# Four-image hybrid network on one core: image 2's gating beside image 3's attention, its output projection in four blocks

## The chip, the cores and the metric

The kernel runs on one core of one Trainium2 chip. The core has four compute engines that each work through a queue of their own in order: PE (TensorE, matmuls into PSUM), DVE (VectorE), ACT (ScalarE) and POOL (GpSimd). A fifth, SP (SyncE), issues the DMAs here. The metric is the device time of one execution in microseconds (us). In what follows "image 3" is the last of four images (numbers 0 to 3).

## The reference, cut to what matters

Each of the 4 images is 1024 tokens of 256 channels. It passes layer 0 (norm, projection, 3x3 depthwise convolution, state-space scan with 64 states, norm, projection), layer 1 (three convolutions), layer 2 (masked attention with 8 heads, then a mixture of 8 experts) and layer 3 (state-space scan with 16 states and a gate, then a second mixture of experts). The change touches the parts below.

```python
# layer 2, attention: t = t + _L2_attn_ref(_ln_t(t), ...)
scores = jnp.where(mask, Q @ K.T / sqrt(32), -inf)
attended = softmax(scores) @ V
y = x + attended @ Wo + bo
out = layernorm(y) * gamma + beta
# layer 2, experts: t = t + _L2_ffn_ref(_ln_t(t), ...); 8 experts of 256 x 256 x 256, two best per token
# layer 3, second half of the scan layer (y from the scan over the tokens)
y = y * silu(x_gate)
t = t + y @ W_out + b_out
# layer 3, experts: t = t + _L3_ffn_ref(_ln_t(t), ...)
logits = xf @ gate_w + gate_b
probs = softmax(logits)
top2_vals, top2_idx = top_k(probs, 2)           # cw: weights of the two best, 0 elsewhere
for e in range(8):                              # 256 x 512 x 256 each
    h = gelu(xf @ W1[e] + b1[e])
    acc = acc + cw[:, e:e+1] * (h @ W2[e] + b2[e])
```

## The kernel before, in words

**Stages and scans.** The program is written out by one loop (`run`). It walks through the units of eight scans in the order of `SCANS`: (0,0), (0,1), (3,0), (0,2), (3,1), (0,3), (3,2), (3,3), where the first number is the layer and the second the image. One unit is 128 lanes by 1024 time steps: a load of `dt` into a buffer `dA`, an exponential on ACT, a matmul that spreads the input (`ps_rep`), a product and a scan on DVE into a buffer `h`, a product on POOL, and a matmul that collects the states (`ps_y`). The pool of the scans holds five buffers `dA`, five `h` and two `rows`, of which each scan takes one `rows`.

Between the units the loop advances the other work of the images as Python generators (`advance`): `front` (layer 0 up to its scan), `middle` (the rest of layer 0, layer 1, attention, layer 2's experts, and layer 3 up to its scan) and `last` (layer 3 behind its scan). Each `yield` is a point at which the loop may go back to the scan. So the order on every engine is fixed when the program is built.

**The end of the program.** The last scan, (3,3), needs image 3's `middle`. When the scan (3,2) has run out, `middle(3)` goes on without a scan beside it: attention's heads, the end of attention, layer 2's experts, and `front3`. Four empty units (`DRAIN`) keep the two scans apart.

**What runs beside it.** `ahead(2)` is image 2's layer 3 behind its scan: `back3` (gate and output projection), `moe(3, 2)` up to a mark `END` (norm, routing), and then its experts. In `middle(3)`, `beside(main, other)` alternates one step of `main` with one step of `other`. Before, `main` is only `moe(2, 3)`, image 3's layer-2 experts with their norm and routing. What is left of `ahead(2)` at its end is run up to `END` (`rest`), and the experts of image 2 come later, beside the last scan.

**Names to follow.** `back3` loads the residual rows into `tb_rows` (a `rows` buffer of the scans' pool), then for each of four blocks of 128 channels the gate (`gate_back`) and the scan's result (`y_back`), both in a pool of its own on the left side. POOL adds the bias to `tb_rows` in four instructions and multiplies `y_back` by the gate in eight (128 x 512 each). PE projects in four blocks of two token groups (`project(j)`, eight matmuls of 128 x 256, PSUM tile `ps_o3`, which the trace shows as `ps_o`), and DVE adds each block to `tb_rows` (`add(j)`).

The end of attention is `divided` (reciprocal on DVE, product on POOL, for each half of the channels of each half of the tokens), `projected` (`ps_wo`, added into `y_at`), and `normed` (statistics `lny`, then POOL's product with gamma and add into `tb`). `moe` begins with its norm (`lnm`, into `xnm`), its transposes (`ps_tr`), its logits (`ps_lg`), on POOL the adds `tb<-tb,xnm`, the routing on DVE (`lg`, `r_one`, `r_two`, `cw`), the weights turned (`ps_ct`) and the bias product (`ps_b`). Then comes the loop over the experts: `ps_h`, a gelu on ACT, `ps_e`, and an accumulation on DVE.

The side work shares three PSUM slots: `ps()` hands out the tags `s`, `s`, `acc` in turn, with two buffers of `s` and one of `acc`. When `self.alone` is set, the scores of the heads use the scans' PSUM instead.

Every operation passes through one metering helper, so the profile puts nearly all of them down to line 130; instructions are told apart by the names of their tiles (`x` in the trace is the buffer `x0`, used again for image 2's transposed rows).

Of the kernel before, what the change touches and what calls it, by code (L numbers as in the profile page):

```python
# [1 line left out]

# [14 lines left out]
P = 128  # L17
NB = 4
# [123 lines left out]
class Hybrid:  # L142
# [476 lines left out]
    def run(self):  # L619

        self.done, self.ready = set(), set()
        self.todo, self.stage, self.wait = list(STAGES), None, None
        self.alone, self.reached = False, 0
        nc, tc = self.nc, self.tc
        with tc.tile_pool(name="scan", bufs=1) as mp, tc.tile_pool(
            name="scps", bufs=1, space=PSUM
        ) as psum, tc.tile_pool(name="sdps", bufs=1, space=PSUM) as side, tc.manual_schedule():
            self.side_psum(side)
            self.scan_psum = psum
            self.mask_work, self.sorted = self.setup(), False  # L630
            clock = self.clock = dict.fromkeys(Metered.COST, 0.0)
            self.nc = Metered(nc, clock)
            for n, _ in enumerate(self.scans(mp, psum)):
                now = clock["vector"]
                if n % 2 and clock["gpsimd"] < now:
                    next(self.mask_work, None)
                for e in clock:
                    clock[e] = max(clock[e], now - LAG)
                for _ in range(TICKS):
                    if max(clock.values()) > clock["vector"] + LEAD or self.advance() is None:  # L640
                        break
            while self.advance() is not None:
                pass
            self.nc = nc
        assert not self.todo
# [269 lines left out]
    def scanned(self, key, y, d):  # L915

        yield Wait((key, d))
        for c in range(2):
            self.nc.sync.dma_start(y[64 * c : 64 * c + 64, d, :], self.mem["y", *key, d, c])

    def back0(self, b, tb):


        nc, tc, vec = self.nc, self.tc, self.vec
        with tc.tile_pool(name=f"k{b}", bufs=1, side="right") as sp:
            nc.sync.dma_start(tb, self.image(self.a["x"].rearrange("b h w c -> (b h w) c"), b))
            y = sp.tile([P, DC, L], F32, name="y_back")
            u = sp.tile([P, DC, L], F32, name="u_back")
            w_out = sp.tile([P, DC, C], F32, name="w_out0")

            def fetch(d):
                nc.sync.dma_start(u[:, d, :], self.mem["u", 0, b, d])
                yield from self.scanned((0, b), y, d)

            def skip(d):
                nc.vector.scalar_tensor_tensor(
                    y[:, d, :], u[:, d, :], vec["L0_conv_D_skip"][:, d : d + 1], y[:, d, :],
                    ALU.mult, ALU.add,
                )

            yield 1.0
            yield from fetch(0)
            yield from self.add_rows(tb, self.bout0, TB)
            nc.sync.dma_start(w_out, self.mem[("w_out0",)])
            for d in range(1, DC):
                yield from fetch(d)
                for _ in range(4):
                    yield 0.5
                skip(d - 1)
                yield 1.3  # L950
            for _ in range(4):
                yield 0.5
            skip(DC - 1)
            yield 1.3
            mv = sp.tile([P, TB, 2], F32, name="b0mv")
            got = {}

            def turn(j):
                got[j] = ps = self.ps("ps_yt")
                for d in range(DC):  # L960
                    nc.tensor.transpose(
                        ps[:, d * P : (d + 1) * P], y[:, d, j * P : (j + 1) * P], self.ident
                    )

            def stats(j):
                st = sp.tile([P, 6], F32, tag="b0st", name="b0st", bufs=2)
                nc.vector.bn_stats(st, got.pop(j))
                nc.vector.bn_aggr(mv[:, j, :], st)

            yield from self.pipe(range(TB), turn, stats, cost=1.0)  # L970
            r = self.rstd(sp, mv[:, :, 1], 1e-5, TB, "b0")
            yield 0.8

            def project(j):
                got[j] = ps = self.ps("ps_o")
                for d in range(DC):
                    nc.tensor.matmul(
                        ps[:, :C], lhsT=y[:, d, j * P : (j + 1) * P], rhs=w_out[:, d, :],
                        start=(d == 0), stop=(d == DC - 1),
                    )  # L980

            def add(j):
                nc.vector.scalar_tensor_tensor(
                    tb[:, j, :], got.pop(j)[:, :C], r[:, j : j + 1], tb[:, j, :], ALU.mult, ALU.add
                )

            yield from self.pipe(range(TB), project, add, cost=1.7)
# [275 lines left out]
    def attention(self, b, tb):  # L1263
        nc, tc, vec = self.nc, self.tc, self.vec
        with tc.tile_pool(name=f"at{b}", bufs=1, side="right") as op:
# [56 lines left out]
            with tc.tile_pool(name=f"ab{b}", bufs=1, side="right") as fp:  # L1322
                yield from self.shift(fp, qT, kT, mT, maskT, go, f"large{b}")
            with tc.tile_pool(name=f"ac{b}", bufs=1, side="right") as fp:
                yield from self.all_heads(fp, tb, qT, kT, v, maskT, mT, xa, wo)

    def all_heads(self, fp, tb, qT, kT, v, maskT, mT, xa, wo):
        nc = self.nc

        def divided(raw, sums, c):  # L1330
# [13 lines left out]
        for n in range(len(steps) + 2):  # L1344
# [13 lines left out]
            if n >= 2 and kb == TB - 1 and hp % 2:  # L1358
                then.append(divided(*halves[nh], hp // 2))
                if nh == 0 and hp == 3:  # L1360
                    then.append(self.finished(fp, tb, 0, halves[0][0], xa, wo, "s"))
        for more in then:
            yield from more
        yield from self.finished(fp, tb, 1, halves[1][0], xa, wo)

    def finished(self, fp, tb, nh, att, xa, wo, tag=None):
        y = yield from self.projected(fp, nh, att, xa, wo, tag)
        yield from self.normed(fp, tb, nh, y)

    def large_scores(self, fp, qT, kT, large):  # L1370
# [236 lines left out]
    def moe(self, which, b, tb, side="right", pause=False):  # L1607
# [8 lines left out]
        with ExitStack() as stack:  # L1616
# [22 lines left out]
            with tc.tile_pool(name=f"mg{which}{b}", bufs=1, side=side) as gp:  # L1639
                xn = gp.tile([P, TB, C], F32, name="xnm")  # L1640
                yield from self.norm(gp, tb, TB, xn, "lnm")
                yield from self.turned(xn, TB, xT)
                lg = gp.tile([P, TB, NEXP], F32, name="lg")
                ps = self.ps("ps_lg", (P, TB, NEXP))
                for j in range(TB):
                    for k in range(2):
                        nc.tensor.matmul(
                            ps[:, j, :], lhsT=xT[:, k, j * P : (j + 1) * P],
                            rhs=self.router[which][:, k, :], start=(k == 0), stop=(k == 1),
                        )  # L1650
                yield 3.0
                if which == 2:
                    nc.vector.tensor_copy(lg, ps)
# [5 lines left out]
                if which == 2:  # L1659
                    for j in range(0, TB, 2):  # L1660
                        tj = tb[:, j : j + 2, :]
                        nc.gpsimd.tensor_tensor(tj, tj, xn[:, j : j + 2, :], ALU.add)
                        yield 0.6
                yield from self.route(gp, lg, cw, which == 2)

                cT = gp.tile([NEXP, L], F32, name="cT")

# [26 lines left out]
            if pause:  # L1694
                yield END
                begin()
            hidden_of = {}
            got = {}

# [222 lines left out]
                    steps = self.beside(steps, self.other, lambda: ("parts", *key, 0) in self.ready)  # L1922
                yield from steps

    def back3(self, b, tb, side="right"):
        nc, tc = self.nc, self.tc
        with tc.tile_pool(name=f"h{b}", bufs=1, side=side) as sp:
            nc.sync.dma_start(tb, self.mem["t", b])
            y = sp.tile([P, DC, L], F32, name="y_back")
            gate = sp.tile([P, DC, L], F32, name="gate_back")  # L1930

            def fetch(d):
                nc.sync.dma_start(gate[:, d, :], self.mem["gate", b, d])
                yield from self.scanned((3, b), y, d)

            def gated(d):
                for g in range(2):
                    cols = slice(g * 512, (g + 1) * 512)
                    nc.gpsimd.tensor_tensor(y[:, d, cols], y[:, d, cols], gate[:, d, cols], ALU.mult)
                    yield 0.8  # L1940

            yield 1.0
            yield from fetch(0)
            w_out = self.weight(sp, "L3_attn_W_out", DC)
            yield from self.add_rows(tb, self.bout3, TB)
            for d in range(1, DC):
                yield from fetch(d)
# [8 lines left out]
            def project(j):  # L1956
                got[j] = ps = self.ps("ps_o3", (P, 2, C))
                for i in range(2):
                    m = 2 * j + i
                    for d in range(DC):  # L1960
                        nc.tensor.matmul(
                            ps[:, i, :], lhsT=y[:, d, m * P : (m + 1) * P], rhs=w_out[:, d, :],
                            start=(d == 0), stop=(d == DC - 1),
                        )

# [1 line left out]
                tj = tb[:, 2 * j : 2 * j + 2, :]  # L1967
                nc.vector.tensor_tensor(tj, got.pop(j), tj, ALU.add)

            yield from self.pipe(range(TB // 2), project, add, cost=3.4)  # L1970

# [37 lines left out]
    def middle(self, b):  # L2011

        with self.tc.tile_pool(name=f"t{b}", bufs=1, side="right") as tp:
            tb = tp.tile([P, TB, C], F32, name="tb")
            yield from self.back0(b, tb)
            yield from self.layer1(b, tb)
            yield from self.attention(b, tb)
            moe = self.moe(2, b, tb)
            if b < NB - 1:
                yield from moe  # L2020
            else:
                self.other = self.ahead(b - 1, "left", self.scan_pool)
                yield from self.rest((yield from self.beside(moe, self.other)))
            yield from self.front3(b, tb)

    def some(self, other, n):
# [28 lines left out]
    def ahead(self, b, side, pool=None):  # L2055

        with ExitStack() as stack:
            if pool is None:
                pool = stack.enter_context(self.tc.tile_pool(name=f"e{b}", bufs=2, side=side))
            tb = pool.tile([P, TB, C], F32, tag="rows", name="tb_rows", bufs=2 if pool is self.scan_pool else 1)  # L2060
            yield from self.back3(b, tb, side)
            yield from self.moe(3, b, tb, side, True)
            self.nc.sync.dma_start(self.image(self.out, b), tb)
            yield 1.0
# [60 lines left out]
```

## Time and profile before

| what | us |
|---|---|
| median of 3 timed runs (lowest, highest) | 6339.24 (6334.23, 6351.4) |
| the profiled execution | 6326.47 |
| its span | 6324.7 |
| PE busy (share) | 5136.2 (81%) |
| DVE busy (share) | 5039.6 (80%) |
| POOL busy (share) | 3824.8 (60%) |
| ACT busy (share) | 3410.2 (54%) |

The granted PE clock is 0.841 of full speed in the mean. The end of the execution divides like this (busy times from the trace, us):

| stretch | what runs | PE | DVE | POOL | clock |
|---|---|---|---|---|---|
| 5120 to 5238 | end of scan (3,2), image 3's attention up to its heads | 94.2 | 99.5 | 70.0 | 0.78 |
| 5240 to 5398 | image 3's heads, no scan | 155.6 | 14.4 | 9.5 | 1.00 |
| 5398 to 5459 | end of attention, norm and routing of the experts; image 2's fetches and gating | 29.2 | 25.9 | 26.0 | 0.58 |
| 5459 to 5601 | image 3's layer-2 experts; image 2's projection, norm and routing | 140.2 | 41.7 | 0.0 | 0.97 |
| 5601 to 5690 | `front3` of image 3 | 77.8 | 7.4 | 0.0 | 0.94 |
| 5690 to 6000 | scan (3,3), image 2's layer-3 experts | 274.4 | 252.9 | 192.9 | 0.95 |
| 6000 to 6324 | image 3's layer 3 to the end | 303.3 | 49.9 | 2.5 | 0.94 |

How to read it: a stretch is as long as the engine or the chain of waits that ends last in it, whatever the share over the whole span. An engine whose busy time comes near to the stretch's length sets it. Where none does, the length comes from instructions on different engines that wait for one another. The clock is the share of its full rate that PE was granted; a low one makes the same matmuls longer.

### The profile page before, as it was taken

Reading aid. Unit: us, or ns where it says so; the run is one execution under the profiler, and the core shown is the slowest. Engines: PE = TensorE matmul, PEld = TensorE weight load, DVE = VectorE, ACT = ScalarE, POOL = GpSimd, SP = SyncE. Lnnn points to the kernel's source line nnn. Section 1 sums busy time; section 2 is a strip of 40 time slices with the busy share of each in tenths; the row PEclk is TensorE's granted clock in tenths of the full one; section 3 lists DMA queues with packets and bytes.
Section 4 is the critical chain, followed back from the end, with each engine's and each line's share of the span. In section 5 each row is a group of like instructions: output and inputs, shape, how many; then the busy total and the mean of one; then the engine's idle time right before and its main releaser. Section 6 shows DMA issues by size and latency. Waiting matters only on the chain. (4 is left out here: it accounts for less than half of the span.)

```text
span 6324.7 us, 59731 instructions
## 1 busy us (share of the span) xinstructions
PE 5136.2 (81%) x20165; PEld 2118.7 (33%) x20249; DVE 5039.6 (80%) x4016; ACT 3410.2 (54%) x4299; POOL 3824.8 (60%) x1948
## 2 busy tenths in 40 slices
PE   6676785579798568979779969889689779797999
PEld 2222120132253022234225432243145332443566
DVE  5888898988898998889889988899889981317811
ACT  3565655345496435558637735577557544236621
POOL 2787768665686765668767756577857661106600
PEclk7687785589798568979869979989789889899989
DMA  3455555544355666445555675345545750226611
GB/s 110 158 159 165 164 175 187 157 150 133 120 172 178 195 166 164 129 131 187 161 176 181 181 177 158 119 150 195 188 146 175 203 150 11 53 73 179 171 34 34
DMA packets 347916, 934.97 MB, mean 148 GB/s; under 512 B 37748, under 2 KB 120257, under 8 KB 345985
## 3 DMA queue, kind: packets, MB, share of 16 engines
q1 hardware_dynamic: 344880, 928.38, 48.5%
q0 software_dynamic: 2128, 2.13, 0.2%
q8 instruction: 165, 2.70, 0.2%
q14 instruction: 167, 1.36, 0.1%
q10 hardware_dynamic: 576, 0.39, 0.0%
HBM read 841.02 MB, written 92.37 MB: 148 GB/s over the span
## 5 line engine op out<-in xcount | busy, mean ns | idle before, releaser
L130 POOL TENSOR_TENSOR h<-h,rows 128x1024 f32<-128x1024 f32 x1280 | 3023.4, 2365 | 1756.9 <-DVE h L130 1560.4
L130 DVE TENSOR_TENSOR_SCAN h<-dA,ps_rep 128x1024 f32<-128x1024 f32 x1280 | 2924.1, 2284 | 182.1 <-ACT dA L130 53.4
L130 DVE TENSOR_TENSOR ps_rep<-ps_rep,rows 128x1024 f32<-128x1024 f32 x1280 | 1549.0, 1210 | 145.6 <-PE ps_rep L130 144.6
L130 PE MATMUL ps_rep<-S,spread_L_conv_A_log 96*128 96x512 bf16 x2048 | 751.9, 456 | 771.7 <-DVE h L130 726.7
L130 ACT ACTIVATE dA<-dA,A_L_conv_A_log 128x1024 f32<-128x1024 f32 x1024 | 1125.6, 1142 | 442.5 <-DMA dA<-dt 414.0
L130 PE MATMUL ps_y<-h,collect_L_conv_A_log 128*32 128x512 f32 x4096 | 705.4, 742 | 15.5 <-POOL h L130 15.5
L130 PE MATMUL ps_e<-we,h_m 128*128 128x256 f32 x3072 | 709.2, 383 | 8.4 <-ACT h_m L130 8.4
L130 PEld LDWEIGHTS <-spread_L_conv_A_log 96*128 96x128 bf16 x2048 | 159.8, 102 | 1557.4 <-DVE h L130 1243.7
L130 PEld LDWEIGHTS ps_e<-we,h_m 128*128 128x128 f32 x3072 | 583.1, 191 | 159.2 <-issue 30.4
L130 PE MATMUL ps_h<-xTm,we 128*128 128x512 f32 x1280 | 603.3, 606 | 4.6 <-DMA we<-in_L_ffn_W_dram 4.5
L130 ACT ACT_TABLE_LOAD x402 | 515.8, 1283 | 37.6 <-PE ps_h L130 15.6
L130 ACT ACTIVATE h_m<-ps_h,cols 128x512 f32<-128x512 f32 x384 | 257.1, 686 | 437.7 <-PE ps_h L130 435.7
L130 ACT ACTIVATE p<-ps_sc 128x512 f32<-128x512 f32 x404 | 219.3, 595 | 319.7 <-PE ps_sc L130 215.2
L130 ACT ACTIVATE dA<-dA,A_L_attn_A_log 128x1024 f32<-128x1024 f32 x256 | 282.8, 1143 | 146.2 <-DMA dA<-dt 134.8
L130 PEld LDWEIGHTS ps_h<-xTm,we 128*128 128x128 f32 x1280 | 242.2, 193 | 279.2 <-issue 211.2
L130 PE MATMUL ps_rep<-S,spread_L_attn_A_log 96*128 96x512 bf16 x512 | 175.4, 430 | 158.2 <-DVE h L130 136.6
L130 PE MATMUL ps_at<-p,v 128*32 128x512 f32 x1024 | 271.5, 610 | 0.2 <-ACT p L130 0.2
L130 PE MATMUL ps_at<-p,ones 128*32 128x512 f32 x1024 | 271.5, 610 | 0.0
L130 PE MATMUL ps_sc<-qT,kT 32*128 32x512 f32 x808 | 244.5, 655 | 5.8 <-ACT p L130 3.5
L130 DVE SCALAR_TENSOR_TENSOR tb_rows<-ps_e,cw,tb_rows 128x256 f32<-128x256 f32 x128 | 55.7, 477 | 242.4 <-PE ps_e L130 242.2
L130 PE MATMUL ps_cv<-pad,diag 128*128 128x512 f32 x504 | 229.2, 594 | 0.0
L130 PEld LDWEIGHTS ps_y<-h,collect_L_conv_A_log 128*32 128x32 f32 x4096 | 93.9, 118 | 339.9 <-issue 224.3
(347 smaller groups left out, 5472.9 us busy)
## 6 DMA issues: line engine op xcount, KB each, us to landing
dA<-dt SPq DMA_DIRECT2D x1280, 512.0 KB
we<-in_L_ffn_W_dram SPq DMA_DIRECT2D x64, 512.0 KB
parts<-parts SPq DMA_DIRECT2D x60, 384.0 KB
S<-parts SPq DMA_DIRECT2D x90, 256.0 KB
dt<-sp_r SPq DMA_DIRECT2D x64, 256.0 KB
y<-yo SPq DMA_DIRECT2D x128, 128.0 KB
y_back<-y SPq DMA_DIRECT2D x64, 256.0 KB
we<-in_L_ffn_w_dram SPq DMA_DIRECT2D x64, 256.0 KB
```

Source lines behind the costliest of these rows:

```text
L130: return got(*args, **kw)
```

## The change

`middle` of the last image now starts `ahead(2)` beside attention and experts together instead of beside the experts alone. `back3` gets a `pause` mode for this. It first waits until the scan (3,2) has ended. Then it takes its `y_back` blocks and `W_out` from the five `h` buffers and its gate blocks from the `dA` buffers of the scans. The gating runs at once. The projection is cut into three groups, each held back by marks that image 3's work sets in `self.passed`: block 0 is issued when the last head is issued ("heads"), blocks 1 and 2 when attention's projection is ("projected"), block 3 when the logits are ("logits"). The adds of a group are issued when the mark "projected", "normed" or "routed" is set. Image 2's `moe(3, 2)` begins when image 3's loop over the experts begins ("route"). The load of `tb_rows` is issued when `ahead(2)` starts, that is behind attention's weights. `scanned` now takes a list of blocks, which changes nothing for layer 0.

```diff
@@ run, scanned @@
+        self.alone, self.reached, self.passed = False, 0, set()
...
-            self.nc.sync.dma_start(y[64 * c : 64 * c + 64, d, :], self.mem["y", *key, d, c])
+            self.nc.sync.dma_start(y[d][64 * c : 64 * c + 64, :], self.mem["y", *key, d, c])
@@ all_heads, finished, moe: the marks @@
+        self.passed.add(("heads", b))
         for more in then:
             yield from more
...
+        if nh:
+            self.passed.add(("projected", b))
         yield from self.normed(fp, tb, nh, y)
...
                 yield from self.norm(gp, tb, TB, xn, "lnm")
+                self.passed.add(("normed", b))
...
+                self.passed.add(("logits", b))
                 yield 3.0
...
                 yield from self.route(gp, lg, cw, which == 2)
+                self.passed.add(("routed", b))
...
             if pause:
                 yield END
                 begin()
+            self.passed.add(("route", b))
@@ back3 @@
-    def back3(self, b, tb, side="right"):
+    def back3(self, b, tb, side="right", pause=False):
...
             nc.sync.dma_start(tb, self.mem["t", b])
-            y = sp.tile([P, DC, L], F32, name="y_back")
-            gate = sp.tile([P, DC, L], F32, name="gate_back")
+            if pause:
+                yield Wait(((3, b), DC - 1))
+
+            def parts(name, tag):
+                if pause:
+                    return [
+                        self.scan_pool.tile([P, L], F32, tag=tag, name=name, bufs=5) for _ in range(DC)
+                    ]
+                x = sp.tile([P, DC, L], F32, name=name)
+                return [x[:, d, :] for d in range(DC)]
+
+            y, gate = parts("y_back", "h"), parts("gate_back", "dA")
...
-            w_out = self.weight(sp, "L3_attn_W_out", DC)
+            if pause:
+                w_out = self.scan_pool.tile([P, L], F32, tag="h", name="w_out3", bufs=5)
+                w_out = w_out.rearrange("p (k n) -> p k n", k=DC)
+                nc.sync.dma_start(w_out, self.a["L3_attn_W_out"].rearrange("(k p) n -> p k n", p=P))
+            else:
+                w_out = self.weight(sp, "L3_attn_W_out", DC)
...
-            yield from self.pipe(range(TB // 2), project, add, cost=3.4)
+            if pause:
+                for blocks, starts, ends in (
+                    ((0,), "heads", "projected"), ((1, 2), "projected", "normed"),
+                    ((3,), "logits", "routed"),
+                ):
+                    yield from self.until(starts, NB - 1)
+                    for j in blocks:
+                        project(j)
+                        yield 3.4
+                    yield from self.until(ends, NB - 1)
+                    for j in blocks:
+                        add(j)
+                        yield 0.5
+            else:
+                yield from self.pipe(range(TB // 2), project, add, cost=3.4)
+
+    def until(self, *what):
+        while what not in self.passed:
+            yield 0.0
@@ middle @@
-            yield from self.attention(b, tb)
-            moe = self.moe(2, b, tb)
             if b < NB - 1:
-                yield from moe
+                yield from self.attention(b, tb)
+                yield from self.moe(2, b, tb)
             else:
                 self.other = self.ahead(b - 1, "left", self.scan_pool)
-                yield from self.rest((yield from self.beside(moe, self.other)))
+                main = chain(self.attention(b, tb), self.moe(2, b, tb))
+                yield from self.rest((yield from self.beside(main, self.other)))
@@ ahead @@
-            yield from self.back3(b, tb, side)
+            yield from self.back3(b, tb, side, pool is self.scan_pool)
+            if pool is self.scan_pool:
+                yield from self.until("route", NB - 1)
             yield from self.moe(3, b, tb, side, True)
```

More of the change, by code (lines that the diff above doesn't have):

```diff
@@ L1 @@
 from contextlib import ExitStack
+from itertools import chain
 import concourse.bass as bass
@@ L622, in run @@
         self.todo, self.stage, self.wait = list(STAGES), None, None
-        self.alone, self.reached = False, 0
+        self.alone, self.reached, self.passed = False, 0, set()
         nc, tc = self.nc, self.tc
@@ L932, in fetch @@
                 nc.sync.dma_start(u[:, d, :], self.mem["u", 0, b, d])
-                yield from self.scanned((0, b), y, d)
+                yield from self.scanned((0, b), [y[:, k, :] for k in range(DC)], d)
             def skip(d):
@@ L1324, in attention, with all_heads @@
             with tc.tile_pool(name=f"ac{b}", bufs=1, side="right") as fp:
-                yield from self.all_heads(fp, tb, qT, kT, v, maskT, mT, xa, wo)
-    def all_heads(self, fp, tb, qT, kT, v, maskT, mT, xa, wo):
+                yield from self.all_heads(b, fp, tb, qT, kT, v, maskT, mT, xa, wo)
+    def all_heads(self, b, fp, tb, qT, kT, v, maskT, mT, xa, wo):
         nc = self.nc
@@ L1360, in all_heads, with finished @@
                 if nh == 0 and hp == 3:
-                    then.append(self.finished(fp, tb, 0, halves[0][0], xa, wo, "s"))
+                    then.append(self.finished(b, fp, tb, 0, halves[0][0], xa, wo, "s"))
+        self.passed.add(("heads", b))
         for more in then:
             yield from more
-        yield from self.finished(fp, tb, 1, halves[1][0], xa, wo)
-    def finished(self, fp, tb, nh, att, xa, wo, tag=None):
+        yield from self.finished(b, fp, tb, 1, halves[1][0], xa, wo)
+    def finished(self, b, fp, tb, nh, att, xa, wo, tag=None):
         y = yield from self.projected(fp, nh, att, xa, wo, tag)
+        if nh:
+            self.passed.add(("projected", b))
         yield from self.normed(fp, tb, nh, y)
@@ L1928, in back3 @@
             nc.sync.dma_start(tb, self.mem["t", b])
-            y = sp.tile([P, DC, L], F32, name="y_back")
-            gate = sp.tile([P, DC, L], F32, name="gate_back")
+            if pause:
[8 more added lines that the diff above has]
+            y, gate = parts("y_back", "h"), parts("gate_back", "dA")
             def fetch(d):
-                nc.sync.dma_start(gate[:, d, :], self.mem["gate", b, d])
+                nc.sync.dma_start(gate[d], self.mem["gate", b, d])
                 yield from self.scanned((3, b), y, d)
@@ L1938, in gated @@
                     cols = slice(g * 512, (g + 1) * 512)
-                    nc.gpsimd.tensor_tensor(y[:, d, cols], y[:, d, cols], gate[:, d, cols], ALU.mult)
+                    nc.gpsimd.tensor_tensor(y[d][:, cols], y[d][:, cols], gate[d][:, cols], ALU.mult)
                     yield 0.8
@@ L1961, in project @@
                         nc.tensor.matmul(
-                            ps[:, i, :], lhsT=y[:, d, m * P : (m + 1) * P], rhs=w_out[:, d, :],
+                            ps[:, i, :], lhsT=y[d][:, m * P : (m + 1) * P], rhs=w_out[:, d, :],
                             start=(d == 0), stop=(d == DC - 1),
```

## The prediction, made before the changed kernel was run

> **What bounds the kernel now.** I first read the busy table and the slices: PE 81%, DVE 80%, but in slices 34 to 37 (some 5215 to 5690 us) DVE falls to tenths 1, 3, 1, 7 while PE holds 7 or more. There no scan runs: the last scan waits for image 3's middle stage, which is alone on the chip. So I cut that stretch into windows at the points where the work changes; columns are busy us and (x instructions) of PE, PEld, DVE, ACT, POOL, then granted clock, DMA share, GB/s.
>
> ```profile
> 5398.00:5411.00 13.00, 7.61 (x24) 4.80 (x16) 4.04 (x2) 2.44 (x3) 1.26 (x1) 0.74 0.00 1
> 5411.00:5428.00 17.00, 0.00 (x0) 0.00 (x0) 11.54 (x37) 4.68 (x10) 9.89 (x8) 0.59 0.56 164
> 5428.00:5440.40 12.40, 12.13 (x48) 9.99 (x48) 0.00 (x0) 5.84 (x12) 9.33 (x8) 0.50 1.05 263
> 5440.40:5449.60 9.20, 0.03 (x2) 0.06 (x2) 7.94 (x23) 0.26 (x1) 5.47 (x5) 0.50 0.38 84
> 5449.60:5458.50 8.90, 8.90 (x25) 5.98 (x25) 2.08 (x3) 2.43 (x3) 0.00 (x0) 0.50 0.00 0
> 5458.50:5480.90 22.40, 22.40 (x81) 16.48 (x81) 3.97 (x7) 2.06 (x3) 0.00 (x0) 0.93 0.00 1
> ```
>
> The rows are: last head to end of attention's projection; norms; transposes and logits; routing on DVE; weights turned and bias product; start of the expert loop. PE has three holes (6 us in the first row, 17, 9) and is full in the last row. From 5458 to 5601 the chain of waits is PE after PE, and image 2's projection `ps_o` sits in it four times:
>
> ```profile
> 5449.57 1.86 PE ps_ct L130 x8
> 5451.44 7.12 PE ps_b L130 x16
> 5458.56 5.29 PE ps_o L130 x16
> 5463.85 1.72 PE ps_h L130 x4
> 5465.56 3.45 PE ps_o L130 x16
> ```
>
> The timeline shows what makes the holes long (start, duration, instruction):
>
> ```profile
> 5404.88 6.12 PE L130 MATMUL ps_wo<-w_L_attn_Wo,raw 128*128 128x256 f32 x14 [5.39 <-POOL raw L130]
> ...
> 5421.92 4.92 POOL L130 TENSOR_TENSOR tb_rows<-tb_rows,row_L_attn_b_out 128x512 f32<-128x512 f32 x4
> ...
> 5423.20 1.22 DVE L130 TENSOR_SCALAR lnm_v<-lnm_mv 128x8 f32<-128x8 f32 x1
> ...
> 5424.99 0.65 DVE L130 TENSOR_TENSOR lnm_w<-lnm_r 128x8 f32<-128x8 f32 x1 [0.56 <-ACT lnm_r L130]
> 5425.67 1.19 DVE L130 TENSOR_TENSOR lnm_w<-lnm_w,lnm_v 128x8 f32<-128x8 f32 x1
> ...
> 5440.90 2.48 POOL L130 TENSOR_TENSOR y_back<-y_back,gate_back 128x512 f32<-128x512 f32 x2
> 5440.95 1.29 DVE L130 TENSOR_TENSOR lg<-lg,r_mx 128x64 f32<-128x64 f32 x1
> ```
>
> Two things are to be seen. After a hole PE runs at half clock: 14 passes of `ps_wo` take 6.12 us, or 0.437 each, where 16 of `ps_o` take 3.45, or 0.216. And tiny DVE operations that take 0.17 us elsewhere (the same `lnm_v` and `lnm_w` at 5493 to 5498) take 0.65 to 1.2 while POOL works for image 2.
>
> **The change, part by part.** Ends are given as (best, worst) beside my value; minus is a gain.
>
> *1. Fetch and gating move under the heads.* POOL has nothing but seven short operations between 5240.6 and 5403, DMA moves 2 GB/s there, and DVE ends the scan at 5238. The 13 transfers (4.5 MB) took from 5422.0 to about 5444 in the old place; from 5242 they land by some 5265 at the same rate. The four bias adds and eight gatings (12 x 1.26 = 15 us of POOL) stand around the two divisions of the first half (5267, 5312), which PE needs only from 5317. Hidden by 158 us in which PE is 98% busy with heads: 0. The scan's `h` and `dA` buffers are idle until the last scan begins at about 5700. SP's two loads of expert weights now queue behind these transfers, but are needed only at the loop.
>
> *2. `tb_rows` is loaded earlier*, on SP right after Wv, at 5117.3, past the `dA` load of 5119.1. That 1 MB lengthens a DMA burst that ended at 5124 by 1 MB / 262 GB/s = 4 us. Cover: ACT touches the next `dA` only at 5131.43, since it stands 10.1 us before `lnt_r`. I take 0 (0, +4 if the cover fails).
>
> *3. POOL is out of the norm's way.* `lnm_v` 1.22 to 0.17, `lnm_w` 0.65 and 1.19 to 0.17 each: -2.55, all on the chain. In the routing, `lg` 1.29 and 0.41, `r_one` 1.17 and 0.93, each to 0.22: -2.9. The adds of `xnm` remain on POOL, but as four in a row from about 5431.6 they end (5.1 us) before the logits do. That POOL is the cause I read from the ends: `lg` ends at 5442.24, 0.1 us after the first of the two gatings begun at 5440.90 (1.24 each), while reductions and operations that fall into POOL's pauses take their 0.22. The added `tb_rows` adds run where POOL is idle or DVE has time.
>
> *4. Block 0 between last head and projection.* Eight matmuls, 3.45 us, in the hole 5398.9 to 5404.9 that waits for reciprocal (3.35) and division (1.26). Nothing is late. PE idles 2.1 us instead of 6, so I expect its clock to hold and `ps_wo` to take 14 x 0.216 = 3.0, not 6.12: -3.1 (-3.1, 0). The row for this: 5504 to 5508, PE busy 2.30 of 4, clock 1.00. Its add on DVE (0.69, one input from PSUM) stands among the statistics, on the chain: +0.7.
>
> *5. Blocks 1 and 2 before the norm ends.* Block 1 reuses block 0's PSUM slot, so it waits for that add; both take 6.9 us in a hole of some 12. Their two adds stand on DVE after `lnm_b`, when DVE has nothing until the logits. Cost 0. The 6 us of idling left is enough to cool PE again, so transposes and logits stay at 0.50.
>
> *6. Block 3 beside the routing.* Started cold it takes 5.2 to 6.9 us[...]. The cleaned routing takes 9.16 - 2.9 = 6.3, so the hole shrinks by 2.8 rather than 2.9: +0.1.
>
> *7. The loop loses four projections*: 5.29 + 3 x 3.45 = -15.6. But the clock decides here. [...]16 passes of `ps_b` at 0.235 (its rows at 5537) and a short `ps_ct` make 5.2 instead of 9.0, and the loop starts warm: -15.6 - 3.8 = -19.4. The rows disagree on what counts as busy:
>
> ```profile
> 5432.00:5436.00 4.00, 4.00 (x22) 4.00 (x20) 0.00 (x0) 1.86 (x4) 2.27 (x2) 0.50 1.04 246
> 5436.00:5440.00 4.00, 4.00 (x20) 4.00 (x21) 0.00 (x0) 0.00 (x0) 4.00 (x5) 0.50 1.03 248
> ```
>
> ```profile
> 5512.00:5516.00 4.00, 4.00 (x32) 3.79 (x29) 0.88 (x2) 2.46 (x3) 0.00 (x0) 1.00 0.23 66
> 5516.00:5520.00 4.00, 4.00 (x19) 3.73 (x19) 0.23 (x1) 0.00 (x0) 0.00 (x0) 0.56 0.00 0
> ```
>
> PE was busy 4.00 of 4 with logits and the clock stayed at 0.50 in the first pair, and fell from 1.00 to 0.56 in the second. Narrow work does not hold it. [...]-15.6 + 2.55 - 1.4 = -14.5 (-19.4, -12.2 where bias product and loop start are all cold).
>
> Image 2's norm and routing start some 25 us earlier in the loop, with the same instructions and table loads, and still end inside it: 0.
>
> **Sum**: -2.55 - 2.8 - 3.1 + 0.7 - 14.5 = **-22.3 us**. The profiled execution took 6326.5 (span 6324.7 and 1.8 around it), so it would take about 6304. The three timed runs lie higher, median 6339.2; the same difference gives **6317**.
>
> **Rivals.** *A, the clock holds*[...]: -27.2, 6312. For it, block 3 is dense; against it, the logits' rows. *B, the holes do not give*: `ps_wo` stays cold, loop and bias product too: 0 + 0.7 - 2.55 - 2.2 - 12.2 = -16.3, with the burst of part 2 not covered -12: 6323 to 6327, within what can be told from no change. For it, PE had cooled 5 us after the last head. *C, slower*: a gating on POOL waits for its transfer in front of the first half's second division, and PE, in order, waits at `ps_wo` of 5317. It decides from the point where the last transfer lands after about 5307 (5313.2 less four gatings); to eat the whole gain it must land at 5330, to show as slower at 5350. In the old place the same transfers took 22 us; here they would need over 85, for instance if SP stood before a `dA` slot that does not come free. Then 6339 + 20 = 6359. *D, the blocks are not where they are said to be*: the changed program's order on PE has `ps_o` after the last `ps_at`, twice after `ps_wo`, and after `ps_lg`, so I give it nothing.
>
> **How the numbers follow.** Forecast 0.57, A 0.15, B 0.23, C 0.05. About 0.3% of 6339, 19 us, is what a measurement of this kernel can tell from no change. The forecast, 3 us past it, with some 4 us of spread between medians (the runs of before span 17), is faster in three of four cases: 0.43; A adds 0.15, B 0.05; together 0.63 faster, 0.32 the same, 0.05 slower. The range runs from A's 6312 less 7 for the runs' spread to B's 6327 plus 7: 6305 to 6334.
>
> **What would show it.** `ps_wo` of the second half in about 3 us; no `lnm` or `r_one` operation over 0.3; PE empty for about 6 us before `ps_tr`, not 17; `ps_ct` within 6.6 us of the last logit; no `ps_o` in the expert loop, whose start comes some 9 us and whose end some 22 us earlier against the last head; the heads' end at the same time as now, near 5398. The forecast is wrong if the scan of image 2 ends later than 5241, if a division waits for a gating, or if the loop shrinks by less than 12.

## The result, and the profile after

The changed kernel takes **6299.65 us** (median of 5 runs, 6294.21 to 6307.27), the kernel before, measured beside it, 6339.24 (5 runs, 6331.15 to 6351.4): ratio 0.9935, 95% interval 0.9918 to 0.9953. The profiled execution has a span of 6292.5 us, before 6324.7. The prediction was 6317 with a range from 6305 to 6334: the direction is right, the gain about twice as large as forecast.

The windows of the stretch after the change, cut where the work changes (columns as before: length, then busy us and instructions of PE, PEld, DVE, ACT, POOL, then granted clock, DMA share, GB/s):

```profile
5390.90:5400.00 9.10, 7.17 (x33) 5.99 (x34) 4.04 (x2) 2.44 (x3) 1.26 (x1) 1.00 0.01 2
5400.00:5415.30 15.30, 7.05 (x33) 5.87 (x31) 10.23 (x40) 4.79 (x11) 5.01 (x4) 0.81 0.22 69
5415.30:5427.60 12.30, 12.14 (x49) 10.09 (x50) 0.56 (x1) 5.73 (x11) 4.95 (x4) 0.50 0.01 1
5427.60:5433.90 6.30, 6.30 (x16) 4.94 (x17) 5.05 (x23) 0.26 (x1) 0.00 (x0) 0.54 0.00 0
5433.90:5438.80 4.90, 4.67 (x25) 3.51 (x24) 2.74 (x4) 2.33 (x3) 0.00 (x0) 1.00 0.00 0
5438.80:5457.00 18.20, 18.20 (x60) 11.13 (x60) 8.20 (x31) 5.82 (x9) 0.00 (x0) 1.00 0.05 14
```

PE's first hole is almost filled (7.17 of 9.1), the routing's is full (6.30 of 6.30). Transposes and logits (third row) are unchanged, at half clock. The fifth row is the surprise: `ps_ct` and `ps_b` take 4.9 us at clock 1.00, where the row of before had 8.9 at 0.50, and the loop starts at 1.00 (last row), where it started at 0.93. The chain of waits (start, duration) shows the same:

```profile
5420.97 6.63 PE ps_lg L131 x32
5427.60 6.48 PE ps_o L131 x16
5434.08 0.45 PE ps_ct L131 x4
...
5435.18 3.71 PE ps_b L131 x16
5438.89 7.06 PE ps_h L131 x16
5445.96 3.45 PE ps_e L131 x16
```

To see where time went in every kernel that follows, I read from each timeline when the same instruction starts (for the last head and the last add: when it ends), and took differences. The columns are one profiled execution each; us from the mark above to this one:

| up to | before | gate_only | block3_in_loop | after | after_again |
|---|---|---|---|---|---|
| last head (from the start of the last scan of (3,2)) | 163.02 | 163.02 | 163.02 | 163.02 | 163.02 |
| second add into `y_at` | 12.18 | 11.29 | 9.34 | 9.34 | 9.34 |
| first `xnm` | 16.46 | 13.91 | 14.50 | 14.51 | 14.50 |
| copy of the logits | 12.94 | 12.94 | 12.94 | 12.94 | 12.95 |
| `ps_ct` | 9.13 | 6.22 | 6.22 | 6.28 | 6.23 |
| `ps_b` | 1.80 | 1.80 | 1.79 | 1.27 | 1.26 |
| first matmul of the experts | 7.12 | 7.12 | 7.12 | 3.64 | 3.65 |
| last add of the experts | 143.45 | 140.31 | 128.17 | 128.00 | 124.66 |
| first scan of (3,3) | 110.94 | 110.59 | 110.41 | 113.84 | 110.78 |
| **sum** | 477.04 | 467.20 | 453.49 | 452.84 | 446.39 |

What lies behind the first scan of (3,3) is equal within 3 us in these five. So the changed stretch is 24.2 us shorter in `after` and 30.7 in `after_again`, the same program. The experiments have to say why the middle rows give more than forecast, why the last two differ between executions of one program, and where the rest of the timed 39.6 us is.

### The profile page after: what moved, and what is told of

Read it like the earlier page. It is cut to its first block, busy times and chain, and to the rows that moved or that the text cites. A ratio compares the mean times of both kernels' runs of the same rounds, so it can differ in the third digit from the quotient of the medians.

```text
span 6292.5 us, 59823 instructions
## 1 busy us (share of the span) xinstructions
PE 5142.7 (82%) x20249; PEld 2117.1 (34%) x20249; DVE 5032.7 (80%) x4016; ACT 3410.6 (54%) x4299; POOL 3825.9 (61%) x1948
```

## Experiments

**The two kernels again, unchanged.** before_again:

> The kernel before, unchanged, as a measure of spread. Theory L (the change gains only where it changes the program, about 27 us between the last step of scan (3,2) and the end of image 3's layer-2 expert loop; the other 12 of the measured 40 us come from PE clock phases that differ between executions): 6330 to 6350 us, ratio to before 0.998 to 1.002; that stretch takes 365 us as in the first profile (within 2), while the start of the last scan (3,2) and the time behind the loop move by up to 10 us against the first profile. Theory S (something in the changed program makes the unchanged stages faster too): the first profile's positions come again within 2 us everywhere.

after_again:

> The changed kernel, unchanged, as a measure of spread. Theory L: the stretch from the last step of scan (3,2) to the end of the layer-2 expert loop takes 338 us again (within 2), the scan itself starts anywhere within 10 us of either first profile; the gain over several rounds comes nearer to 27 us than 40 (30 to 35). Theory S: the gain is 38 to 42 us again and the last step of scan (3,2) stands some 8 us earlier than in the kernel before.

Before: 6325.34 us (22 runs), ratio 0.9994 (0.9985 to 1.0002). Changed: 6291.44 (6 runs), ratio 0.9942 (0.9926 to 0.9957). The stretch is 477.13 us in the one and 446.39 in the other, so it repeats to 0.1 us before and varies by 6 after the change, more than the 2 us that were expected. The last scan of (3,2) began at 5227.95 in this execution of before and at 5235.84 in the first, though nothing was changed. The two theories are not parted here: the changed kernel's gain of 38.2 us is what S expected, but its last scan of (3,2) began at 5233.30, not 8 us ahead of before's.

**Gating early, projection back at the loop** (gate_only):

```diff
             if pause:
-                for blocks, starts, ends in (
-                    ((0,), "heads", "projected"), ((1, 2), "projected", "normed"),
-                    ((3,), "logits", "routed"),
-                ):
...
+                yield from self.until("route", NB - 1)
+                yield from self.pipe(range(TB // 2), project, add, cost=3.4)
```

> The changed kernel with its four projection blocks back at the start of the expert loop; gating stays under the heads. My sum: only POOL's absence from norm and routing gains, 2.55 + 2.9 = 5.5 us against before (stretch 359 to 360 us). Rival (the gain comes from moving the fetches and the gating, whose DMA traffic or POOL work slowed more than the rows that were long): 12 us or more, stretch under 354.

6320.4 us (22 runs), ratio 0.9985 (0.9977 to 0.9992). The stretch is 9.8 us shorter than before's, where 5.5 were expected. The norm goes from 16.46 to 13.91 (-2.55) and the routing from 9.13 to 6.22 (-2.91), the two prices of the prediction's third step to 0.01. Most of the other 4.4 us lies in two places that the expectation left out. PE still waits 5.4 us empty before `ps_wo`, which takes 5.24 us instead of 6.12, because the clock rose 4.0 us after the start of these passes and not 5.8. The loop is 3.1 us shorter with the same projection in it: before, a `ps_e` waits 1.80 us there for a gelu that stands on ACT behind image 2's `xnm`, and here this wait is gone; for most of the rest the clock falls for 3.4 us at image 2's logits instead of 6.8.

**Block 3 alone back in the loop** (block3_in_loop):

```diff
-                    ((3,), "logits", "routed"),
...
+                yield from self.until("route", NB - 1)
+                yield from self.pipe((3,), project, add, cost=3.4)
```

> The changed kernel with block 3 of the projection moved from beside the routing to the start of the expert loop. Theory A (the dense block 3 just before it keeps PE's clock up through the turned weights, the bias product and the loop's start): these run at half clock again, 4.2 us for turned weights and bias product, some 2 for the start, and the block itself 3.45, so 9 to 10 us slower than the changed kernel; turned weights and bias product take 9.0 us at clock 0.50. Rival (the clock there was a matter of phase, block 3 has no part in it): 3 to 4 us slower, and turned weights and bias product take about 5 us.

6300.85 us (6 runs), 9.4 above after_again, which was measured beside it. Its stretch is 7.1 us longer (453.49 against 446.39); the other 2 us lie elsewhere. Its timeline (start, duration):

```profile
5432.19 1.86 PE L131 MATMUL ps_ct<-ident,cw 128*8 128x128 f32 x8 [6.25 <-DVE cw L131]
5433.98 7.19 PE L131 MATMUL ps_b<-b,cT 8*128 8x256 f32 x16
5441.10 3.78 PE L131 MATMUL ps_h<-xTm,we 128*128 128x512 f32 x4
5444.68 3.98 PE L131 MATMUL ps_o<-w_out,y_back 128*128 128x256 f32 x16
```

With PE empty for 6.25 us in the routing, `ps_b` takes 7.19 us again instead of 3.71 and the first four passes of `ps_h` take 3.78 us, where the chain of after has 7.06 for sixteen. So block 3 does two things in its new place: the loop is rid of it (3.5 us), and the clock, which rises to 1.00 in after 5.9 us into it, stays there over the 4.9 us behind it (4.0 us). That is rival A of the prediction.

**Block 0 alone back in the loop** (block0_in_loop):

```diff
-                    ((0,), "heads", "projected"), ((1, 2), "projected", "normed"),
+                    ((1, 2), "projected", "normed"),
...
+                yield from self.until("route", NB - 1)
+                yield from self.pipe((0,), project, add, cost=3.4)
```

> The changed kernel with block 0 of image 2's projection moved from between the heads and attention's projection to the start of the experts' loop. If block 0 is what keeps PE's clock up for ps_wo: from the last head to the second add into y_at 11.3 to 12.2 us instead of 9.34, the norm 0.65 shorter (13.85 instead of 14.50, the add of block 0 is gone from it), the loop 3.45 longer: +4.8 to +5.7 us in all. Rival: ps_wo is short because POOL's gatings are gone from its divisions: 9.34 stays, +2.8 us in all.

6306.15 us (6 runs), ratio 0.9957 (0.9941 to 0.9973). To the second add into `y_at` it takes 12.20 us, the norm 13.91, and the cold row is back:

```profile
5418.10 6.15 PE L131 MATMUL ps_wo<-w_L_attn_Wo,raw 128*128 128x256 f32 x14 [5.39 <-POOL raw L131]
```

So block 0 is what keeps `ps_wo` warm (6.15 us here, 3.29 in after), and POOL's missing gatings are not. The loop is 4.0 us longer than after_again's, 3.45 expected. In this execution the clock fell within `ps_b` (4.44 us) although block 3 stood before it, and the loop started at 0.50: holding the clock is not certain (the last section compares the executions). With this the stretch is 6.9 us longer than after_again's, where 4.8 to 5.7 were expected.

**The bias adds of `tb_rows` beside the norm** (bias_beside_norm), without a transfer there:

```diff
-            yield from self.add_rows(tb, self.bout3, TB)
+            if not pause:
+                yield from self.add_rows(tb, self.bout3, TB)
...
                     yield from self.until(ends, NB - 1)
+                    if ends == "normed":
+                        for _ in self.add_rows(tb, self.bout3, TB):
+                            pass
```

> The changed kernel with the four bias adds of tb_rows on POOL put back beside the second norm, without any transfer there. Theory (POOL's work slows the tiny DVE operations beside it): lnm_v and lnm_w take 0.6 to 1.2 us again instead of 0.17, the norm (second add into y_at to first xnm) 17.0 us instead of 14.50. Rival (the transfers of 164 to 263 GB/s slowed them): 14.50 stays. POOL's adds tb<-tb,xnm start some 1.3 us later and still end before the logits, so nothing else changes: +2.5 us or 0, seen in the trace rather than in the time.

6305.48 us (13 runs), ratio 0.9961 (0.9949 to 0.9972). The norm is 17.07 us. The timeline:

```profile
5414.26 4.92 POOL L131 TENSOR_TENSOR tb_rows<-tb_rows,row_L_attn_b_out 128x512 f32<-128x512 f32 x4
...
5415.54 1.23 DVE L131 TENSOR_SCALAR lnm_v<-lnm_mv 128x8 f32<-128x8 f32 x1
...
5417.33 0.65 DVE L131 TENSOR_TENSOR lnm_w<-lnm_r 128x8 f32<-128x8 f32 x1 [0.56 <-ACT lnm_r L131]
5418.02 1.19 DVE L131 TENSOR_TENSOR lnm_w<-lnm_w,lnm_v 128x8 f32<-128x8 f32 x1
```

In after, without POOL beside them, the same three take 0.17 us:

```profile
5412.94 0.17 DVE L131 TENSOR_SCALAR lnm_v<-lnm_mv 128x8 f32<-128x8 f32 x1
5413.68 0.17 DVE L131 TENSOR_TENSOR lnm_w<-lnm_r 128x8 f32<-128x8 f32 x1 [0.56 <-ACT lnm_r L131]
5413.88 0.17 DVE L131 TENSOR_TENSOR lnm_w<-lnm_w,lnm_v 128x8 f32<-128x8 f32 x1
```

In bias_beside_norm POOL's four adds end at 5415.52, 5416.74, 5417.96 and 5419.18. `lnm_v` ends at 5416.77, the two `lnm_w` at 5417.98 and 5419.20: each stays until the POOL instruction of its time ends. DMA moved 1 GB/s there (5414 to 5421), so the cause is POOL's work, not transfers. The same profile also has `ps_wo` cold behind block 0:

```profile
5397.76 4.97 PE L131 MATMUL ps_wo<-w_L_attn_Wo,raw 128*128 128x256 f32 x14 [1.93 <-POOL raw L131]
```

It is the same wait of 1.93 us as in after, where `ps_wo` took 3.29:

```profile
5396.85 3.29 PE L131 MATMUL ps_wo<-w_L_attn_Wo,raw 128*128 128x256 f32 x14 [1.93 <-POOL raw L131]
```

**More dense work before the transposes** (warm_norm): blocks 1 and 2 are computed twice into the same PSUM.

```diff
-                    for d in range(DC):
+                    for d in [*range(DC)] * (2 if pause and j in (1, 2) else 1):
```

> The changed kernel with each matmul row of blocks 1 and 2 computed twice, 7 us more of dense work in PE's hole before the transposes (same output). PE is then busy up to 1.3 us before ps_tr. If only idling cools PE: transposes follow ACT's xnm at 0.49 each and the logits take 3.65 us, so from first xnm to the logits' copy 8.5 to 9.5 us instead of 12.94: -4 us. If narrow or sparse work cools it too (ps_tr at ACT's pace, 128x8 logits): the logits still start at half clock or fall to it, 11 to 12 us: -1 to -2. If the hole was not the cause: 12.94, 0. Block 3 behind the logits starts warm in the first case (3.5 us) and leaves 2.7 us empty before ps_ct: ps_ct and ps_b stay at 4.9, or go back to 8.9 if that cools it.

6309.3 us (16 runs), ratio 0.9969 (0.996 to 0.9979). From first `xnm` to the copy of the logits it takes 12.94 us, no gain: the third of the expected outcomes, but not for its reason. The windows:

```profile
5426.00:5428.00 2.00, 2.00 (x10) 1.43 (x8) 1.30 (x7) 0.42 (x2) 0.00 (x0) 1.00 0.00 0
5428.00:5430.00 2.00, 0.43 (x3) 0.23 (x2) 1.82 (x6) 1.24 (x3) 0.07 (x1) 1.00 0.00 0
5430.00:5432.00 2.00, 1.79 (x5) 0.72 (x5) 0.00 (x0) 2.00 (x5) 2.00 (x2) 0.60 0.00 0
...
5434.00:5438.00 4.00, 4.00 (x21) 4.00 (x19) 0.00 (x0) 1.17 (x2) 0.88 (x1) 0.50 0.01 4
5438.00:5442.00 4.00, 4.00 (x19) 3.99 (x19) 0.27 (x2) 0.00 (x0) 0.00 (x0) 0.50 0.00 0
5442.00:5446.00 4.00, 4.00 (x11) 3.11 (x10) 3.23 (x15) 0.26 (x1) 0.00 (x0) 0.50 0.00 0
5446.00:5450.00 4.00, 3.77 (x19) 2.80 (x18) 2.23 (x9) 1.36 (x3) 0.00 (x0) 0.82 0.00 0
```

The clock is 1.00 up to 5430 and falls during the first transposes, which come one by one behind ACT's `xnm`. Then PE counts as busy 4.00 of 4 with 128 x 8 logits for two windows, and the clock stays at 0.50; it rises only some 6 us into block 3. Warming PE up to 1.4 us before sparse, narrow work bought nothing.

**Image 2's logits spread among the experts** (lg_spread, and again as lg_spread_again). In the loop these 32 passes of 128 x 8 stand in one row. In two executions of the changed kernel they read:

```profile
5472.00 4.69 PE L131 MATMUL ps_lg<-wr,x 128*128 128x8 f32 x32
5476.54 3.76 PE L131 MATMUL ps_e<-we,h_m 128*128 128x256 f32 x8
```

```profile
5477.43 3.63 PE L131 MATMUL ps_lg<-wr,x 128*128 128x8 f32 x32
5480.92 1.97 PE L131 MATMUL ps_e<-we,h_m 128*128 128x256 f32 x8
```

The first pair is after, the second after_again: in the one the clock falls under the logits, and the dense `ps_e` behind them is still at half rate. With the half-rate start of the `ps_h` that follows (4.14 us for eight passes, 3.60 when warm) this makes up the 3.3 us between 128.00 and 124.66. The edit puts a step of the experts between each two pairs of matmuls (four passes), with the scans' PSUM, idle there:

```diff
-                ps = self.ps("ps_lg", (P, TB, NEXP))
+                if pause and b < NB - 1:
+                    ps = self.scan_psum.tile([P, L], F32, tag="x", name="ps_lg", bufs=2)
+                    ps = ps[:, : TB * NEXP].rearrange("p (j n) -> p j n", j=TB)
+                else:
+                    ps = self.ps("ps_lg", (P, TB, NEXP))
                 for j in range(TB):
+                    if pause and b < NB - 1 and j:
+                        yield 0.5
```

> The changed kernel with image 2's logits in the experts' loop cut into eight pairs of matmul rows with an expert's step between each two, so that they never fill a stretch of 4 us (their PSUM is the scans'). If these narrow matmuls cool PE's clock in some executions and not in others: the loop takes 124.7 us (as in one look of the changed kernel) and not 128.0 (as in the other), no window of the loop is under 1.00, and the time is 0 to 3 us below the changed kernel's. Rival (the 3.3 us come from elsewhere): 128.0 again is possible, with windows under 1.00 at another place.

> Image 2's logits spread among the experts, a second look. Loop 124.7 us and all of its windows at 1.00 if the narrow logits were what cooled PE there; 128.0 if that was chance. Time 0 to 3 us below the changed kernel's, within the scatter of medians.

6297.86 us (7 runs, ratio 0.9955, 0.9939 to 0.9971) and 6297.76 (6 runs, 0.9944, 0.9929 to 0.996). In the first the loop takes 124.66 us with every window at 1.00. In the second it takes 126.36, which the expectation did not have; the clock is 1.00 at all logits, and the 1.7 us are a loop start at half clock:

```profile
5438.75 8.83 PE L131 MATMUL ps_h<-xTm,we 128*128 128x512 f32 x16
...
5473.63 0.51 PE L131 MATMUL ps_lg<-wr,x 128*128 128x8 f32 x4
```

Logits in one row cooled PE in eight of the eleven profiles that have them so, spread logits in neither of two. That is in favour of the theory; the last section shows in which executions the clock falls. A gain in time is not shown: lg_spread_again is 10.6 us below after_third, which was measured beside it, but their stretches are equal (449.6 and 449.8 us).

**Both kernels a third time**, to settle where the rest of the timed difference comes from (before_third, after_third):

> The kernel before, unchanged. For the profile: last scan of (3,2) to first scan of (3,3) 477 us again; the scan (3,2) ends anywhere within 5226 to 5250, as in the ten profiles so far. Time: ratio 1.

> The changed kernel, unchanged. Last scan of (3,2) to first scan of (3,3) between 446.4 (no window of the experts' loop and of front3 at half clock) and 452.9 us. If the gain is local and the rest of the timed difference is how PE's clock falls in the scans before (theory L), the median is 24 to 31 us below that of before within the scatter of some 8 us that medians of the same program show, and the scans end within 5226 to 5250 with no shift against before. If the unchanged stages are faster too (theory S): 34 to 40 below again, and scans that end some 8 us earlier than before's.

Before: 6330.28 us (14 runs), stretch 477.05. Changed: 6308.37 (6 runs), ratio 0.9961 (0.9949 to 0.9973), stretch 449.83, 27.2 shorter. The last scan of (3,2) began at 5247.73 in this execution of the changed kernel, 12 to 20 us later than in before's three. The gain is 26.1 us against the runs of before measured beside it. So nothing speaks for unchanged stages that are faster (theory S). Over the 13 profiles this point lies between 5226 and 5249; before's three and the changed kernel's three overlap (5228 to 5236 and 5228 to 5248).

## Why the prediction was right in direction and wrong in size

Its steps, with before's and after's rows of the table:

- **1 and 2, fetch, gating and the early load cost nothing**: the last head comes 163.02 us after the last scan in every one of the 13 profiles. The early load costs nothing either: the last 45 scans of (3,2), in which it falls, take 211.27 to 211.40 us in the three profiles of before and 211.27 to 211.34 in the three of the changed kernel. The sign that the prediction set, a scan that ends later than 5241, came in after_third (at 5250) without such a cost: the place of the scan scatters more than the sign allowed for.
- **3, POOL out of the way, -2.55 and -2.9**: -2.55 and -2.91 in gate_only. Right, and so is its cause (bias_beside_norm).
- **4, block 0, -3.1 for `ps_wo` and +0.7 for the add**: -2.84 and +0.60. Right in size, though not in every execution: `ps_wo` was partly cold once in the eight profiles that have block 0 in its new place.
- **5, blocks 1 and 2, 0**: the transposes and logits stay at 12.94. Right (PE stood empty before them for 8.3 us where some 6 were forecast, which cost nothing).
- **6, block 3 sets the routing's length, +0.1**: 6.28 against 6.22 (started cold, block 3 took 6.63 us). Right.
- **7, the loop without four projections**: -15.6 by count, -15.45 measured in after. But its clock term failed, and this is the step of the sum that was wrong: the 2.55 for a cold start of the experts and the -1.4 for `ps_ct` and `ps_b` with a clock that falls behind block 3 were my estimate, which no row showed. In after the clock held: `ps_ct` and `ps_b` took 4.91 us instead of 8.92 (-4.0), and the start was warm. The term is -4.0 where the sum had +1.15. The rows that I let decide, logits at 1.00 falling to 0.56, were about 128 x 8 matmuls; `ps_b` with its 256 columns was let go with them. In the eight profiles with block 3 in the routing, `ps_ct` and `ps_b` were warm to their end in six and the experts' start in five. The cold start that I forecast exists, in three of eight.

With step 7 mended the prediction's own sum is **rival A's -27.2**, to which it gave 0.15. The three executions of the changed kernel have -24.2, -30.7 and -27.2 in this stretch (mean -27.4). They differ by the clock at two places that the prediction took as fixed: image 2's logits in the loop (cooled before the change in all three profiles of before; not in after_again: -3.3 more) and `front3`, where after lost 2.9 us against before: 1.9 to a clock that rose 10.1 us after the start of the transposes and not 6.9, 1.0 to one that was at 0.50 for 6.8 us and not 3.4 at the `ps_h` of image 2 behind `ps_dt`.

The **base** was the larger error. The three timed runs of before had a median of 6339.2, and the prediction laid its difference on it. All 132 timed runs of before have a median of 6330.3 and a standard deviation of 8.6; the changed kernel's 17 runs have 6299.7 and 8.0. Of the miss of 17 us, 9 are that base (6339.2 - 6330.3), 5 step 7 (27.2 - 22.3), and 3 the difference between -27.2 and the pooled difference of -30.6. The uncertainty of the latter would be some 4 us if all runs were independent (1.96 times the root of 8.0 squared / 17 + 8.6 squared / 132). It is larger: the changed kernel's runs came in three groups with medians of 6291.4, 6299.7 and 6308.4, which differ by 6 to 13 us inside. These 3 us are therefore within the uncertainty. The range took 7 us for the runs' spread, for medians of three and five runs of a program whose single runs spread by 40.

The rivals: A is what happened. B (holes do not give) is excluded by -2.84, -2.55, -2.85 and the clock of 1.00 behind block 3. C (a gating waits for its transfer) and D did not occur: no head moved.

## What to carry to other kernels

Work of PE that is moved into a wait for another engine can pay twice: it leaves its old place, and the clock can be up for what follows the wait (block 3: 3.5 and 4.0 us; blocks 1 and 2 gave only the first). Fill the last microseconds before the dependent matmuls (block 3 ran in the 6.48 us before `ps_ct`), and price both. Narrow matmuls are to be watched: in one row they did not raise the clock here (0.50 through some 7 us of them in warm_norm) and did not surely hold it, while spread between dense ones they held it in both profiles. Before laying a difference on a base of three runs, ask how far single runs scatter: where unchanged stages move by 20 us, a gain of 27 is read from the changed stretch in the profile, not from two medians.

## What the hardware showed that was not expected

Executions of one program differ in steps, and the one step that was examined is the granted clock. Its record in the 13 traces has a pattern. It is 1.00 or 0.50, and within a trace every change lies on one grid of 3.413 us (173 changes in before, 167 in after, each within 0.03 us of it). How the program lies on this grid differs between executions: `ps_wo` behind block 0, after the same wait of 1.93 us, began 2.4 us before a point of the grid in after and took 3.29 us; in bias_beside_norm it began 0.6 us before one, at which the clock fell, and took 4.97. For image 2's logits in one row the place on the grid is what parts the eight profiles from the three: the clock fell at the end of a grid step that held 2.34 us of logits or more, and stayed where no step held more than 2.30 us (at most 1.02 when they are spread). The margin is thin, and no run moves it on purpose in one row. The steps of after and then of after_again, with the busy us of `ps_lg` alone (PE, PEld, DVE, then clock, DMA share, GB/s):

```profile
5470.94:5474.35 3.41, 2.35 (x22) 2.54 (x23) 0.00 (x0) 1.00 0.00 0
5474.35:5477.77 3.42, 2.34 (x12) 2.24 (x11) 0.23 (x1) 0.50 0.00 0
```

```profile
5476.31:5479.72 3.41, 2.29 (x22) 2.48 (x22) 0.00 (x0) 1.00 0.00 0
5479.73:5483.14 3.41, 1.33 (x12) 1.24 (x12) 0.23 (x1) 1.00 0.01 2
```

Behind block 3 it is alike. Where the clock rose at most 0.6 us before `ps_ct` (six profiles), `ps_b` ran warm; in block0_in_loop and bias_beside_norm it rose 2.7 and 3.1 us before, and fell within `ps_b`.

The 1216 scans up to the end of (3,2) take the same time within 1 us in 56 of 80 stretches of 15 and differ in a few by 3 to 8.5 us (most in the one that begins at some 2412 us); with these the 13 profiles reach the end of (3,2) up to 23 us apart. That stretch is image 1's attention beside a scan, the same instructions in both programs. Windows of before and then of after there:

```profile
2470.00:2474.00 4.00, 4.00 (x14) 0.84 (x14) 0.63 (x1) 1.09 (x2) 1.15 (x1) 0.50 0.00 0
2474.00:2478.00 4.00, 4.00 (x16) 0.68 (x16) 2.89 (x2) 1.08 (x2) 0.83 (x1) 0.50 0.00 0
```

```profile
2468.00:2472.00 4.00, 4.00 (x28) 1.03 (x26) 3.52 (x2) 1.08 (x2) 2.33 (x1) 1.00 0.00 0
2472.00:2476.00 4.00, 4.00 (x22) 1.17 (x24) 1.36 (x2) 2.92 (x5) 2.35 (x1) 1.00 0.49 100
```

PE is busy throughout in both, with 14 to 16 matmuls in 4 us at half clock in the one and 22 to 28 at full clock in the other; two scans later before has lost 7.8 us against after. The whole cost of the stretches at half clock was not measured here. What differs between executions, up to 23 of 6300 us or 0.4%, is as large as the whole effect of this change.
